# Four graph layers in fp32: layer normalisation folded into centred weight matrices and PSUM evictions

## The chip, the cores and the metric

The kernel runs on one core of a Trainium2 chip. The metric is the device time of one execution in microseconds; the figure used is the median of the runs shown. Engines are named as in the profile: PE is TensorE's matmul stream and PEld its weight loads, DVE is VectorE, ACT is ScalarE, POOL is GpSimd, SP is SyncE, which here issues most of the DMA transfers. PSUM is the memory that TensorE writes its products to; other engines read ("evict") it from there.

## The reference

Everything is fp32. There are N = 2708 rows with D = 256 columns in `x` and a weighted adjacency matrix `adj` of N x N. Four layers follow each other, each a graph step and a feed-forward step, both on a layer normalisation without parameters and both added back:

```python
def _layernorm(x, axis=-1, eps=1e-5):
    m = jnp.mean(x, axis=axis, keepdims=True)
    v = jnp.var(x, axis=axis, keepdims=True)
    return (x - m) / jnp.sqrt(v + eps)

x = x + gnn(_layernorm(x), adj)        # layers 0 to 3
x = x + ffn(_layernorm(x))
```

- Layer 0: `gnn` is `weights @ (x @ W + B)`, weights an exponential of adj; `ffn` is a mixture of 8 experts, top 2, hidden size 1024.
- Layer 1: `gnn` is `relu(A @ (x @ W) + b)` with `A = adj + I`, its entry (i, j) scaled by deg_i and deg_j, deg being one over the root of the row sum; `ffn` is one hidden layer of 1024 and one of 8 output matrices for each row.
- Layer 2: `gnn` is a one-head graph attention: `h = x @ W.T`, scores `a_src[j] + a_dst[i]`, leaky ReLU, softmax over the neighbours, `elu(w @ h)`; `ffn` has routed experts of hidden size 512 and a layer normalisation with gamma and beta of its own at its end.
- Layer 3: `gnn` is the same with 4 heads of 64 columns; `ffn` is a linear map, `x @ weight.T + bias`.

With the row's mean m and rstd = 1/sqrt(v + eps), a normalised row times a matrix W is rstd * ((x - m) @ W). It is also rstd * (x @ C), where C is W with the mean of each of its columns taken off, because x @ C = x @ W - m * (column sums of W). Both kernels compute the same values in exact arithmetic.

## The kernel before

`x` stays on the chip as 22 tiles of 128 rows (the last has 20). TensorE contracts over partitions, so each tile must be turned before a product with a weight matrix: two transposes of 128 x 128 (one for each half of the 256 columns, `DC` = 2) into PSUM (line L203), and one copy out of it on ACT (L204), all in `turn_to`. `times` then issues the products of a tile (L246; an fp32 matmul leaves two records). Tiles go through in `FOURS`: the first two, then five groups of four. `stats` gives mean and variance of a group (L176, L177 on DVE) and, with `by_log`, rstd by a logarithm and an exponential on ACT (L141). `shift` makes nb = -mean * rstd (L195). ACT then writes the normalised tile xn = rstd * x + nb.

Where this stands in the program, in order of time:

- **Layer 0** (0 to 612 us). Its first weight matrix is already centred, by two products with a matrix of ones and two DVE steps (L821 to L826). Its `x` goes in without xn. The graph product is L891; experts follow (L587 to L689).
- **Layer 1's front** (613.7 to 672). `norm_project` goes through FOURS. `both` loads the two expert outputs of two tiles ("both", from DRAM, in the four places of the tag "adrow" in pool `gp`), and DVE adds them to x (L1037). Then stats, shift, xn (L215), transposes and copy, products, and ACT's eviction to `sup` with scale `deg` (L1100). The graph product follows, L1164: for each of 22 row blocks of adj a load (L1129, tag "adrow"), a mask (L1133), the diagonal (L1136, L1137), and products into PSUM `acc`. `Units` (the experts) own three places `hs` in one tile of the pool `hw`, set to zero at the start (L621), into which rows are gathered (`fetch_rows`, L638).
- **Layer 2's front** (1140 to 1176.5). For each four: a load "mine" and the add (L1284), `norm_stretch` (L229 to L240, xn L235), products with `w_l2` (256 columns and two score columns), a copy of the scores (`sc`, L1293), row scores turned and sent through DRAM (L1208, L1210), exponentials, and `hh` = product times an exponential (L1301, DVE). The attention product is L1367, with weights `e` from DVE (L1361).
- **Layer 3's parts** (1400 to 1590). The feed-forward step of layer 2 goes over parts of up to four tiles: hidden L353 and L355, `outputs` L1550 to L1554. One part later `finish` normalises y, applies gamma and beta, adds to x (L1566, L1584 to L1586), takes the statistics of x and writes the normalised x into `y` (L1579); `front` turns it, multiplies by `wa` (256 + 8 columns) and evicts three pieces on ACT (L1604 to L1606). The last part's finish and front are written as a generator, `last_stretch`, that is worked off step by step inside the attention (`waiting`, L1741).
- **Layer 3's attention** (1590 to 1951). For slots of (turn, row block): DVE makes e (L1753), PE multiplies into num (L1783) and den (L1793). `closing`, another generator, finishes 16 tiles inside it: ELU, statistics, xn (L1727), the last product with `wf`, bias and x (L1735, L1736), and the output's DMA. `close` and `last` do it for the last six tiles after the attention (`norm_stretch`, POOL's bias add L1676, o L1680, DMA L1681).

Each engine works off its own queue in order. The builder chooses the order of the instructions in a queue, within the program's data dependences; `behind`, `pin`, `after` and `add_manual_dep` add to these by hand. The adds of `both` are held behind the last entry of `shifts` in this way.

Of the kernel before, what the change touches and what calls it, by code (L numbers as in the profile page):

```python
# [8 lines left out]
F32 = mybir.dt.float32  # L9
# [57 lines left out]
def adj_ffn4(ctx: ExitStack, tc: tile.TileContext, a: dict, out: bass.AP):  # L67
# [138 lines left out]
    def norm_project(pool, w_sb, emit, ahead=None, by_log=False):  # L206
        for tiles in FOURS:
            if ahead is not None:
                ahead(tiles)
            st = stats(tiles, by_log=by_log)  # L210
            nb = shift(st, len(tiles))
            for i, t in enumerate(tiles):
                r = rows(t)
                xn = work.tile([P, D], F32, name="xn")[:r]
                s.activation(xn, x[:r, t, :], AF.Identity, scale=st[1][:r, i : i + 1],  # L215
                             bias=nb[:r, i : i + 1])
                xT = pool.tile([P, DC, P], F32, name="xT", bufs=3)
                turn_to(xT[:, :, :r], xn, r)
                emit(t, r, times(xT, 0, r, w_sb, D))
# [6 lines left out]

    def norm_stretch(xT, c0, w, by_log=False):

        own = tiles_of(c0, w)  # L229
        st = stats([t for t, _, _ in own], by_log=by_log)  # L230
        nb = shift(st, len(own)) if by_log else None
        for i, (t, k, r) in enumerate(own):
            xn = work.tile([P, D], F32, name="xn")[:r]
            if by_log:
                s.activation(xn, x[:r, t, :], AF.Identity, scale=st[1][:r, i : i + 1],  # L235
                             bias=nb[:r, i : i + 1])
            else:
                norm_to(xn, t, i, st)
            turn_to(xT[:, :, k : k + r], xn, r)
        return own  # L240
# [369 lines left out]
    class Units(Blocks):  # L610
# [3 lines left out]
        def __init__(self, pool, given, weights, hidden):  # L614
# [5 lines left out]
            self.hs = pool.tile([P, 3, HC * P], F32, name="hs")  # L620
            g.memset(self.hs, 0.0)  # L621
# [12 lines left out]
        def fetch_rows(self):  # L634
            m, n = self.named.pop(0)
            h = self.hs[:, self.places[1] % 3, :]
# [112 lines left out]
    with ExitStack() as l0:  # L749
# [71 lines left out]
        p = ps_tmp()  # L821
        for c in range(DC):
            te.matmul(p[:, :D], lhsT=all_ones, rhs=w_sb[:, c, :], start=(c == 0), stop=(c == DC - 1))
        for c in range(DC):
            v.scalar_tensor_tensor(w_sb[:, c, :], p[:, :D], -1.0 / D, w_sb[:, c, :], op0=ALU.mult,
                                   op1=ALU.add)  # L826
# [26 lines left out]
        for tiles in GROUPS:  # L853
# [8 lines left out]
            for j in range(FULL):  # L862
# [5 lines left out]
                if begin and j % 2 == 0:  # L868
                    for t0 in (j,) if j < FULL - 3 else (j, j + 2) if j == FULL - 3 else ():
                        front(t0)  # L870
# [127 lines left out]
    with ExitStack() as l1:  # L998
# [25 lines left out]
        def both(tiles):  # L1024

            for t0 in tiles[::2]:
                two = range(t0, min(t0 + 2, tiles[-1] + 1))
                o = gp.tile([P, 2, 2 * D], F32, name="both", tag="adrow", bufs=4)
# [18 lines left out]
        def send1(tiles):  # L1047
# [44 lines left out]
            for i, t in enumerate(tiles):  # L1092
# [6 lines left out]
        norm_project(gp, w_l1,  # L1099
                     lambda t, r, p: s.activation(sup[:r, t, :], p, AF.Copy,  # L1100
                                                  scale=deg[:r, t : t + 1]), both, True)
# [89 lines left out]
        def beside(b):  # L1191
            if b == NA + 4:
# [5 lines left out]
                score_columns(w_l2, D, ad_bc, 1, D + 1)  # L1198

# [38 lines left out]
    with tc.tile_pool(name="t3", reuse_waits="tile", bufs=1) as t3:  # L1238
# [29 lines left out]
        with tc.tile_pool(name="g2", reuse_waits="tile", bufs=1) as gp:  # L1268
# [5 lines left out]
            for tiles in FOURS:  # L1274
# [11 lines left out]
                own = norm_stretch(xT, t0 * P, (n - 1) * P + rows(tiles[-1]), True)  # L1286
# [4 lines left out]
                for i, (t, k, r) in enumerate(own):  # L1291
                    ps.append(times(xT, k, r, w_l2, D + 2, ps_acc()))
                    s.copy(sc[:r, i, :], ps[-1][:, D:])  # L1293
# [6 lines left out]
                for p, (t, k, r) in zip(ps, own):  # L1300
                    v.tensor_scalar(hh[:r, t, :D], p[:, :D], hh[:r, t, D :], None, op0=ALU.mult)  # L1301
# [51 lines left out]
            for n in (5, 5, 5, 4, 2):  # L1353
# [18 lines left out]
                if c0 == 0:  # L1372
                    score_columns(wa, D, row_bc(work, "L3_gnn_a_r", D, "elu_e"), NH, D)
                    score_columns(wa, D, row_bc(work, "L3_gnn_a_l", D, "elu_e"), NH, D + NH)

# [124 lines left out]
        with tc.tile_pool(name="h2", reuse_waits="tile", bufs=2) as hp:  # L1500
# [56 lines left out]
            def finish(own, y, by_log=False):  # L1557
# [17 lines left out]
                st = stats(tiles, by_log=by_log)  # L1575
                yield
                nb = shift(st, len(own))
                for i, (t, q0, r) in enumerate(own):
                    s.activation(y[:r, i, :], x[:r, t, :], AF.Identity, scale=st[1][:r, i : i + 1],  # L1579
                                 bias=nb[:r, i : i + 1])  # L1580
# [7 lines left out]
            def front(own, y, c0, w):  # L1588

                sc = gp.tile([P, 4, NH], F32, name="sc", bufs=1)  # L1590
# [3 lines left out]
                def turn(i, r):  # L1594
                    xTs.append(gp.tile([P, DC, P], F32, name="xT3", bufs=3))
                    turn_to(xTs[i][:, :, :r], y[:r, i, :], r)

                turn(0, own[0][2])
                for i, (t, k, r) in enumerate(own):
# [4 lines left out]
                    s.copy(wh[:r, t, :, :DK], p[:, :D].rearrange("p (h d) -> p h d", h=NH))  # L1604
                    s.copy(wh[:r, t, :, DK], p[:, D : D + NH])
                    s.copy(sc[:r, i, :], p[:, D + NH :])  # L1606
# [14 lines left out]
            for c0, w in parts:  # L1621
# [9 lines left out]
                if was is not None:  # L1631
                    at_once(finish(*was[:2], end))
                y = ypool.tile([P, 4, D], F32, name="y", bufs=2)
                outputs(own, hT, y)
                if was is not None:
                    at_once(front(*was))
                    for t in range(NT) if was[2] == 0 else ():
# [4 lines left out]
                was = (own, y, c0, w)  # L1642
        sums.close()

        with tc.tile_pool(name="g3e", reuse_waits="tile", bufs=1) as ge, ExitStack() as sums:
# [22 lines left out]
            def last(tiles):  # L1668

                for g0 in range(0, len(tiles), 4):  # L1670
# [3 lines left out]
                    own = norm_stretch(xT, c0, some[-1] * P + rows(some[-1]) - c0, True)  # L1674
                    for t, k, r in own:
                        g.tensor_tensor(x[:r, t, :], x[:r, t, :], bf[:r], ALU.add)  # L1676
                    for t, k, r in own:
                        p = times(xT, k, r, wf, D)
                        o = work.tile([P, D], F32, name="o")
                        v.tensor_tensor(o[:r], p, x[:r, t, :], ALU.add)  # L1680
# [201 lines left out]
```

## Time and profile before

| what | us |
|---|---|
| median of 3 runs (1965.44 to 1976.37) | 1967.63 |
| the profiled execution | 1973.19 |
| its span, first to last instruction | 1971.4 |
| busy: PE / PEld | 1859.3 / 1349.5 |
| busy: DVE / ACT / POOL | 1087.3 / 678.5 / 324.3 |
| L203 to L246, the front of layer 1 | 621.5 to 672.0 |
| first L1284 to first L1367, the front of layer 2 | 1140.4 to 1176.5 |
| last L1550 to first L1783 | 1581.3 to 1590.2 |
| last attention product to the end of the span | 1950.7 to 1971.4 |

The profile is of one execution, so its parts add up to its own time, 1973.19 us. Busy time counts the time in which an engine executes, not that in which it waits for another. The chain of waits follows the work that ended last back from the end: what stands on it sets the time. The clock granted to TensorE varies between half and full speed, and a product takes about twice as long at half: four records of L246 in layer 1's front took 2.09 us at 0.50 and 1.13 to 1.14 at 1.00.

### The profile page before, as it was taken

How to read it: one execution, taken by the hardware profiler on the slowest of the kernel's cores; microseconds unless marked ns; L12 is line 12 of the kernel's file. 1: busy time of each engine (PE TensorE's matmuls, PEld its weight loads, DVE VectorE, ACT ScalarE, POOL GpSimd, SP SyncE). 2: the span in 40 equal slices, each digit the busy share in tenths (PEclk: the TensorE clock that was granted, in tenths of full speed). 3: DMA queues.
4: the chain of work that ended last, by engine and by line, in shares of the span. 5: the costliest groups of instructions: out<-in, count | busy, mean ns of one | idle time of the engine just before them, and what ended most of it. 6: DMA issues, size and time to landing. Idle time of an engine off the chain costs nothing.

```text
span 1971.4 us, 26038 instructions
## 1 busy us (share of the span) xinstructions
PE 1859.3 (94%) x9613; PEld 1349.5 (68%) x9613; DVE 1087.3 (55%) x2460; ACT 678.5 (34%) x1560; POOL 324.3 (16%) x361
## 2 busy tenths in 40 slices
PE   7999989999997999999897879999899999999997
PEld 6888778888886788888786758888566732232343
DVE  7686852543334324443441165456364399899896
ACT  7878832222223303113131261224243452032232
POOL 1005363333321000201436400000000000000000
PEclk9999989999996999999898989999899999999999
DMA  8536477887753352533758830000101000000000
GB/s 270 153 98 170 130 260 277 324 319 267 292 226 121 107 155 98 146 104 114 232 181 275 306 87 1 1 1 1 43 1 33 17 1 23 22 11 28 20 20 15
DMA packets 87141, 243.95 MB, mean 124 GB/s; under 512 B 17139, under 2 KB 41163, under 8 KB 77792
## 3 DMA queue, kind: packets, MB, share of 16 engines
q1 hardware_dynamic: 70048, 197.09, 30.2%
q0 software_dynamic: 16960, 45.12, 6.8%
q8 instruction: 79, 1.29, 0.3%
q14 instruction: 54, 0.44, 0.1%
HBM read 216.29 MB, written 28.71 MB: 124 GB/s over the span
## 4 chain that ended last, share of the span: by engine, by line
PE 73%; DMA 11%; DVE 7%; issue 4%; ACT 3%; POOL 1%; SPq 0%; POOLq 0%; DVEq 0%; ACTq 0%
PE num L1783 10%; PE ps_acc L1367 9%; PE acc L1164 8%; PE ps_tmp L353 8%; PE acc L891 7%; PE den L1793 5%; PE ps_acc L587 5%; PE yacc L597 5%; PE ps_tmp L246 4%; DMA given<-ys,xs 4%; PE ps_acc L1550 3%; DMA given<-ys,names 1%; DMA hs<-hid,names 1%; PE ps_tmp L203 1%; PE yacc L688 1%
## 5 line engine op out<-in xcount | busy, mean ns | idle before, releaser
L1753 DVE SCALAR_TENSOR_TENSOR e<-arena,G,mask 128x1024 f32<-128x1024 f32 (+1 forms) x264 | 287.7, 1148 | 18.3 <-PE den L1793 18.3
L1783 PE MATMUL num<-e,wh 128*64 128x512 f32 (+4 forms) x1056 | 214.9, 551 | 0.3 <-ACT L_gnn_W L1210 0.3
L1367 PE MATMUL ps_acc<-hh,e 128*128 128x257 f32 x882 | 199.2, 382 | 1.7 <-ACT o L1312 1.7
L1164 PE MATMUL acc<-sup,adrow 128*128 128x256 f32 x882 | 199.6, 383 | 1.1 <-DMA adrow<-in_adjT 1.1
L891 PE MATMUL acc<-msg,wt 128*128 128x256 f32 x882 | 197.7, 381 | 1.9 <-DVE wt L851 1.2
L1164 PEld LDWEIGHTS acc<-sup,adrow 128*128 128x128 f32 x882 | 166.0, 191 | 28.7 <-issue 4.9
L1367 PEld LDWEIGHTS ps_acc<-hh,e 128*128 128x128 f32 x882 | 163.6, 190 | 29.3 <-ACT o L1312 4.7
L891 PEld LDWEIGHTS acc<-msg,wt 128*128 128x128 f32 x882 | 164.9, 190 | 27.2 <-DVE wt L851 2.1
L589 ACT ACTIVATE hTs<-ps_acc,wa 128x256 f32<-128x256 f32 (+1 forms) x192 | 88.8, 466 | 245.9 <-PE yacc L597 166.8
L587 PE MATMUL ps_acc<-xTs,wa 128*128 128x256 f32 (+1 forms) x768 | 170.8, 375 | 1.9 <-DVE xTs L560 1.8
L597 PE MATMUL yacc<-wb,hTs 128*128 128x256 f32 x736 | 167.4, 380 | 1.8 <-DVE ys L599 1.8
L587 PEld LDWEIGHTS ps_acc<-xTs,wa 128*128 128x128 f32 x768 | 137.5, 191 | 28.9 <-DVE xTs L560 5.4
L1783 PEld LDWEIGHTS num<-e,wh 128*64 128x64 f32 (+1 forms) x1056 | 66.3, 136 | 127.6 <-issue 108.0
L597 PEld LDWEIGHTS yacc<-wb,hTs 128*128 128x128 f32 x736 | 137.5, 190 | 20.1 <-DVE ys L599 2.5
L1361 DVE SCALAR_TENSOR_TENSOR e<-Rb,G,mask 128x640 f32<-128x640 f32 (+2 forms) x110 | 85.1, 774 | 92.8 <-PE ps_acc L1367 92.7
L204 ACT COPY xT<-ps_tmp 128x256 f32<-128x256 f32 x120 | 41.8, 364 | 229.5 <-PE ps_tmp L203 228.9
L1793 PE MATMUL den<-e,wh 128*32 128x512 f32 (+4 forms) x1056 | 118.0, 548 | 0.0
L1133 DVE TENSOR_SCALAR mask<-adrow 128x1024 uint8<-128x1024 f32 (+1 forms) x66 | 41.4, 629 | 127.9 <-DMA adrow<-in_adjT 127.7
L688 PE MATMUL yacc<-wb,hTs 128*128 128x256 f32 x384 | 94.4, 397 | 7.9 <-DMA wb<-in_L_ffn_Wdp 7.5
L688 PEld LDWEIGHTS yacc<-wb,hTs 128*128 128x128 f32 x384 | 74.1, 200 | 19.9 <-issue 4.8
L851 DVE SCALAR_TENSOR_TENSOR wt<-adrow,wt 128x640 f32<-128x640 f32 (+3 forms) x67 | 71.0, 1062 | 29.3 <-ACT wt L141 29.0
L1793 PEld LDWEIGHTS den<-e,wh 128*32 128x32 f32 (+1 forms) x1056 | 30.2, 108 | 77.9 <-issue 73.8
(446 smaller groups left out, 2632.4 us busy)
## 6 DMA issues: line engine op xcount, KB each, us to landing
adhalf<-in_adjT SPq DMA_DIRECT2D x42, 677.0 KB
wb<-in_L_ffn_W2p SPq DMA_DIRECT2D x24, 1152.0 KB
wb<-in_L_ffn_Wdp SPq DMA_DIRECT2D x24, 1152.0 KB
wa<-in_L_ffn_W1b SPq DMA_DIRECT2D x24, 1028.0 KB
adrow<-in_adjT SPq DMA_DIRECT2D x42, 512.0 KB
adrow<-in_adjT SPq DMA_DIRECT2D x42, 320.0 KB
adrow<-in_adjT SPq DMA_DIRECT2D x21, 576.0 KB
hid<-hrow POOLq DMA_DIRECT2D x21, 512.0 KB, 3.6
```

Source lines behind the costliest of these rows:

```text
L353: te.matmul(p[:, :w], lhsT=w1[:, c, f * P : (f + 1) * P], rhs=xnT[:, c, c0 : c0 + w], start=(c == 0), stop=(c == DC - 1))
L587: te.matmul(p[:, f % 2, : m * P], lhsT=w1[:, c, f * P : (f + 1) * P], rhs=xT[:, c, : m * P], start=(c == 0), stop=(c == DC - 1))
L589: s.activation(hT[:, f, : m * P], p[:, f % 2, : m * P], AF.Gelu, bias=bias[:, f : f + 1])
L597: te.matmul(q[:, k, :], lhsT=hT[:, f, k * P : (k + 1) * P], rhs=w2[:, f, :], start=(f == 0), stop=(f == HC - 1))
L688: te.matmul(q, lhsT=hT[:, f, :], rhs=w2[:, f, :], start=(f == 0), stop=(f == HC - 1))
L891: te.matmul(p[:q, n - pair[0], :], lhsT=wt[:, k : k + q], rhs=msg[:r, j, :], start=(j == 0 and n == pair[0]), stop=(j == FULL - 1 and n == ...
L1164: te.matmul(p[:q, n - pair[0], :], lhsT=ad[:, k : k + q], rhs=sup[:r, j, :], start=(j == 0 and n == pair[0]), stop=(j == FULL - 1 and n == ...
L1361: v.scalar_tensor_tensor(e[:r, :w], Rb[:r, c0 : c0 + w], G[:r, j, :], mask[:r, j, c0 : c0 + w], op0=ALU.max, op1=ALU.mult)
L1367: te.matmul(p[:, : D + 1], lhsT=e[:, k : k + q], rhs=hh[:, j, :], start=(j == 0), stop=False)
L1753: v.scalar_tensor_tensor(e[:, :w], slow[:, m % 2, k, :w], G[:, j, 2 * pair + k, :], mask[:, j, c0 : c0 + w], op0=ALU.max, op1=ALU.mult)
L1783: te.matmul(num[k * DK : (k + 1) * DK, hf, :q], lhsT=wh[some, j, 2 * pair + k, :DK], rhs=e[some, h0 - c0 : h0 - c0 + q], start=(j == 0), s ...
L1793: te.matmul(den[z : z + Q, :q], lhsT=wh[some, i, 2 * pair + k, DK : DK + 1] .to_broadcast([some.stop - some.start, Q]), rhs=e[some, h0 - c ...
```

## The change

1. `norm_project` becomes `project`. It transposes x itself, two tiles into one PSUM bank, with one ACT copy for both (512 wide), ahead of the statistics. `by` = rstd * deg (DVE) is the scale of the eviction to `sup`. xn and nb go.
2. The centring of layer 0 becomes a function, `centre`, and is also used for the matrices of layer 1 (`w_l1`, inside layer 0's graph product), layer 2 (`w_l2`, among layer 1's units), layer 3 (`wa`, at the start of layer 2's product) and the last one (`wf`, in a generator that starts at slot 19 of the attention).
3. `hs` becomes three tiles with the tag "hs" in `hw`, and `both` loads into that tag; "adrow" is used by rows of adj only.
4. Layer 2's front turns x itself; the scores are evicted with scale rstd, and `hh` takes rstd as a second factor.
5. `finish` no longer writes the normalised x; `front` turns x, and its three evictions are scaled by rstd.
6. `last` and `closing` turn x; rstd is a factor in the step that makes o. In `closing`, mean and xn go.

The diff, cut to its core:

```diff
-    def norm_project(pool, w_sb, emit, ahead=None, by_log=False):
+    def project(pool, w_sb, scale, ahead, emit):
         for tiles in FOURS:
-            if ahead is not None:
-                ahead(tiles)
-            st = stats(tiles, by_log=by_log)
-            nb = shift(st, len(tiles))
+            ahead(tiles)
+            t0, G = tiles[0], len(tiles)
+            turned = []
+            for i in range(0, G, 2):
+                xT = pool.tile([P, DC, 2 * P], F32, name="xT", bufs=2)
+                p = ps_tmp()
+                r = rows(t0 + i + 1)
+                for k in range(2):
+                    q = rows(t0 + i + k)
+                    for c in range(DC):
+                        te.transpose(p[:, (c * 2 + k) * P : (c * 2 + k) * P + q],
+                                     x[:q, t0 + i + k, c * P : (c + 1) * P], ident[:q, :q])
+                s.copy(xT[:, :, : P + r], p.rearrange("p (c t) -> p c t", c=DC)[:, :, : P + r])
+                turned.append(xT)
+            st = stats(tiles, by_log=True)
+            by = small.tile([P, G], F32, name="by", tag=f"by{G}", bufs=2)
+            shifts.append(v.tensor_tensor(by, st[1], scale[:, t0 : t0 + G], ALU.mult).ins.name)
             for i, t in enumerate(tiles):
                 r = rows(t)
-                xn = work.tile([P, D], F32, name="xn")[:r]
-                s.activation(xn, x[:r, t, :], AF.Identity, scale=st[1][:r, i : i + 1],
-                             bias=nb[:r, i : i + 1])
-                xT = pool.tile([P, DC, P], F32, name="xT", bufs=3)
-                turn_to(xT[:, :, :r], xn, r)
-                emit(t, r, times(xT, 0, r, w_sb, D))
+                emit(t, r, times(turned[i // 2], i % 2 * P, r, w_sb, D), by[:r, i : i + 1])
+
+    def centre(w):
+        n = w.shape[2]
+        p = ps_tmp()
+        for c in range(DC):
+            te.matmul(p[:, :n], lhsT=all_ones, rhs=w[:, c, :], start=(c == 0), stop=(c == DC - 1))
+        for c in range(DC):
+            v.scalar_tensor_tensor(w[:, c, :], p[:, :n], -1.0 / D, w[:, c, :], op0=ALU.mult,
+                                   op1=ALU.add)
...
-            self.hs = pool.tile([P, 3, HC * P], F32, name="hs")
-            g.memset(self.hs, 0.0)
+            self.hs = [pool.tile([P, HC * P], F32, name="hs", tag="hs", bufs=3) for _ in range(3)]
+            for h in self.hs:
+                g.memset(h, 0.0)
...
                 if begin and j % 2 == 0:
+                    if j == 6:
+                        centre(w_l1)
...
-                o = gp.tile([P, 2, 2 * D], F32, name="both", tag="adrow", bufs=4)
+                o = hw.tile([P, 2, 2 * D], F32, name="both", tag="hs", bufs=3)
...
-        norm_project(gp, w_l1,
-                     lambda t, r, p: s.activation(sup[:r, t, :], p, AF.Copy,
-                                                  scale=deg[:r, t : t + 1]), both, True)
+        project(gp, w_l1, deg, both,
+                lambda t, r, p, by: s.activation(sup[:r, t, :], p, AF.Copy, scale=by))
...
                 score_columns(w_l2, D, ad_bc, 1, D + 1)
+                centre(w_l2)
...
-                own = norm_stretch(xT, t0 * P, (n - 1) * P + rows(tiles[-1]), True)
+                own = tiles_of(t0 * P, (n - 1) * P + rows(tiles[-1]))
+                for t, k, r in own:
+                    turn_to(xT[:, :, k : k + r], x[:r, t, :], r)
+                rstd = stats(tiles, by_log=True)[1]
...
-                    s.copy(sc[:r, i, :], ps[-1][:, D:])
+                    s.activation(sc[:r, i, :], ps[-1][:, D:], AF.Copy, scale=rstd[:r, i : i + 1])
...
-                for p, (t, k, r) in zip(ps, own):
-                    v.tensor_scalar(hh[:r, t, :D], p[:, :D], hh[:r, t, D :], None, op0=ALU.mult)
+                for i, (p, (t, k, r)) in enumerate(zip(ps, own)):
+                    v.tensor_scalar(hh[:r, t, :D], p[:, :D], rstd[:r, i : i + 1], hh[:r, t, D :],
+                                    op0=ALU.mult, op1=ALU.mult)
...
                     score_columns(wa, D, row_bc(work, "L3_gnn_a_l", D, "elu_e"), NH, D + NH)
+                    centre(wa)
...
-                st = stats(tiles, by_log=by_log)
-                yield
-                nb = shift(st, len(own))
-                for i, (t, q0, r) in enumerate(own):
-                    s.activation(y[:r, i, :], x[:r, t, :], AF.Identity, scale=st[1][:r, i : i + 1],
-                                 bias=nb[:r, i : i + 1])
+                rstd.append(stats(tiles, by_log=by_log)[1])
                 yield
...
-                    turn_to(xTs[i][:, :, :r], y[:r, i, :], r)
+                    turn_to(xTs[i][:, :, :r], x[:r, own[i][0], :], r)
...
-                    s.copy(wh[:r, t, :, :DK], p[:, :D].rearrange("p (h d) -> p h d", h=NH))
-                    s.copy(wh[:r, t, :, DK], p[:, D : D + NH])
-                    s.copy(sc[:r, i, :], p[:, D + NH :])
+                    one = by[:r, i : i + 1]
+                    s.activation(wh[:r, t, :, :DK], p[:, :D].rearrange("p (h d) -> p h d", h=NH),
+                                 AF.Copy, scale=one)
+                    s.activation(wh[:r, t, :, DK], p[:, D : D + NH], AF.Copy, scale=one)
+                    s.activation(sc[:r, i, :], p[:, D + NH :], AF.Copy, scale=one)
...
-                    own = norm_stretch(xT, c0, some[-1] * P + rows(some[-1]) - c0, True)
+                    own = tiles_of(c0, some[-1] * P + rows(some[-1]) - c0)
+                    by = stats(some, by_log=True)[1]
+                    for t, k, r in own:
+                        turn_to(xT[:, :, k : k + r], x[:r, t, :], r)
...
-                        v.tensor_tensor(o[:r], p, x[:r, t, :], ALU.add)
+                        v.scalar_tensor_tensor(o[:r], p, by[:r, i : i + 1], x[:r, t, :], op0=ALU.mult,
+                                               op1=ALU.add)
...
-                v.scalar_tensor_tensor(mv[:q, 0:1], mv[:q, 0:1], -1.0, mv[:q, 1:2], op0=ALU.mult,
-                                       op1=ALU.mult)
-                xn = work.tile([P, D], F32, name="xn")[:q]
-                s.activation(xn, x[:q, t, :], AF.Identity, scale=mv[:q, 1:2], bias=mv[:q, 0:1])
-                yield
                 xT = gp.tile([P, DC, P], F32, name="xT3", bufs=3)
-                turn_to(xT[:, :, :q], xn, q)
+                turn_to(xT[:, :, :q], x[:q, t, :], q)
...
-                v.tensor_tensor(o, p, bf[:q], ALU.add)
+                v.scalar_tensor_tensor(o, p, mv[:q, 1:2], bf[:q], op0=ALU.mult, op1=ALU.add)
...
+            def centred():
+                centre(wf)
+                yield
...
-            scores, active, waiting = {}, [], [(1, last_stretch())]
+            scores, active, waiting = {}, [], [(1, last_stretch()), (19, centred())]
```

## The prediction

> **What bounds the kernel now.** I read the page first (engine shares, the forty slices), then the chain of waits, then tables by stretch for the places that the diff touches.
>
> ```profile
> PE 1859.3 (94%) x9613; PEld 1349.5 (68%) x9613; DVE 1087.3 (55%) x2460; ACT 678.5 (34%) x1560; POOL 324.3 (16%) x361
> PE   7999989999997999999897879999899999999997
> PEclk9999989999996999999898989999899999999999
> PE 73%; DMA 11%; DVE 7%; issue 4%; ACT 3%; POOL 1%; SPq 0%; POOLq 0%; DVEq 0%; ACTq 0%
> ```
>
> TensorE is busy for 94% of the span and carries 73% of the chain. So ACT work that the diff deletes (88 normalisations of 0.6 us, 53 us in all) is worth its own time nowhere in general; it counts where TensorE waits. Slice 13 (591 to 641 us) has the lowest clock of all, 0.6: there the front of layer 1 begins. The stretches of that front (columns: PE, PEld, DVE, ACT, POOL busy, clock, DMA share, GB/s):
>
> ```profile
> 620.00:628.00 8.00, 5.50 (x13) 3.33 (x14) 5.49 (x17) 4.11 (x11) 0.00 (x0) 0.50 0.83 282
> 628.00:636.00 8.00, 6.50 (x17) 4.17 (x17) 6.74 (x22) 4.95 (x13) 0.00 (x0) 0.50 0.59 167
> 640.00:644.00 4.00, 2.93 (x12) 2.00 (x12) 2.22 (x5) 2.92 (x8) 0.00 (x0) 0.79 0.00 0
> 644.00:652.00 8.00, 5.57 (x27) 3.93 (x26) 6.00 (x23) 5.33 (x14) 0.00 (x0) 1.00 0.56 168
> 660.00:668.00 8.00, 8.00 (x43) 6.61 (x42) 1.21 (x3) 4.57 (x12) 0.00 (x0) 1.00 0.22 66
> ```
>
> TensorE had half its clock until 640 and gaps until 652; from 660 it never waits. Why it waits is in the chain (start, length, what):
>
> ```profile
> 629.03 2.09 PE ps_tmp L246 x4
> 631.14 0.47 ACT sup L1100
> 631.61 0.33 ACT xT L204
> 631.95 0.04 issue
> 631.99 2.09 PE ps_tmp L246 x4
> ...
> 1582.65 1.48 ACT y L1579 x3
> 1584.12 0.27 ACT xT L204
> 1584.43 2.13 PE ps_tmp L246 x4
> ...
> 1958.60 0.61 ACT xn L235
> 1959.20 0.04 issue
> 1959.25 0.69 PE num L203 x2
> ```
>
> One tile is product, eviction, copy of the next transposes, product: 2.96 us at half clock, 1.95 at full. The other two places show TensorE behind a normalisation: at the end of layer 3's parts and at the kernel's end.
>
> **Layer 1's front (L1037, L215, L203, L246).** Removed: 22 xn (603 ns each on ACT) and five nb (163 ns). Moved: transposes go ahead of the statistics, two tiles share one copy, so products no longer alternate with one copy and one eviction. Added: five small multiplications (`by`). Work per four tiles: DVE 2.49 (adds) + 2.2 (statistics) + 0.16, and in the new order also the mask, ident and diag of an adj row (0.69 + 0.29 + 0.23) ahead of `by`: about 6.1, 6.5 with waits. TensorE at full clock takes 4 x (0.87 + 0.22) = 4.4, at half 8.7; ACT 4 x 0.47 + 2 x about 0.6 = 3.1. With DVE as the limit, the five `by` after 621.3 end at about 629, 635, 641.5, 647 and 652.6 and the last sup at 655.2. Of the products L1164 the old order holds 34 records (17 products, 0.435 us each) inside the front, the new one 5; so 12 x 0.435 = 5.2 us must be added for the same point: 660.4 against 672.0, a gain of 11.6. The added wait is that of sup for `by`; behind it on ACT stand the next pair's copy and so the next transposes, and the products' PSUM banks stay taken: four banks serve both, so TensorE stalls when DVE is some two tiles late, which is why I let DVE set the pace. Bounds: 4 if DVE waits for the first adj rows, 16 if it never does.
>
> SP's order: both0 to 3, adj row 0, both4 and 5, row 1 and so on. `both` gets three places of its own instead of four shared ones; each load waits for the add three loads earlier. Old transfers ended by 640 at up to 282 GB/s, and both are read in tile order, so I cost this at nothing; if that cover fails, a load takes 3.98 us (the first one) and shifts the chain by part of that. The memsets of the units' three `hs` tiles now wait for the last adds, on POOL (2.7 us); behind them are only gathers needed near 757, so nothing. After the front TensorE is the limit (8.00 of 8).
>
> *The clock.* The trace shows 0.50 for 28 us although PE was busy for 69 to 88% of each stretch; in layer 2's front 0.50 became 0.65 and 1.00 within about 4 us, during four transposes and eight products without a gap. [...]
>
> **Layer 2's front (L1284, L1293, L1301; 1140.4 to 1176.5).** 22 xn and nb go; transposes start after the adds at 1141.1 instead of 1143.5 (2.4 us). The cycle per four tiles is 5.7 us (L1208 at 1153.66, 1159.49, 1165.16). DVE then has 1.25 + 2.27 + 1.8 (hh) = 5.3 of it. DVE's hh of the last tiles are queued behind the first e's, with the first product waiting; that is inside the lower bound. hh takes a second factor inside the same instruction, and sc a scale (its copy is 170 ns; bound -0.02 to +0.1 each). First product 1173.7 instead of 1176.5: gain 3 (1 to 5).
>
> **Layer 3's parts (1403 to 1590).** TensorE runs back to back through 13.7 us of L353 and 13.8 of L1550, and the y at L1579 hide beside it; deleting them gives nothing there. The three evictions per tile become scaled activations. The nearest rows:
>
> ```profile
> L1604 ACT COPY wh<-ps_tmp 128x256 f32<-128x256 f32 x19 | 7.0, 370 | 8.6 <-PE ps_tmp L246 8.6
> L1100 ACT ACTIVATE sup<-ps_tmp,deg 128x256 f32<-128x256 f32 x21 | 10.0, 474 | 18.9 <-PE ps_tmp L246 18.9
> ```
>
> So +0.1 for the large one, and for the two small ones between nothing and +0.1. TensorE waits 0.64 to 1.33 us before L1208 for these evictions; +0.2 to 0.5 a front, five fronts: a loss of 1.5 (1 to 2.5). At the last part, TensorE idles from 1581.28 to 1583.19 for y: x is complete on DVE at 1580.2, so 1.9 come back; the following products run at half clock (2.13), and part of 2.5 more comes with a shorter idle time. Late next is rstd for the eviction, near 1582.2. Gain 3.5 (2 to 4.4). The last stretch inside the attention waits 1.65 us (1613.9 to 1615.5) for the same y, but DVE is full there (9.8 of 10): gain 1 (0 to 1.7).
>
> **Attention and closing.** From 1640 to 1945 PE is busy 20.00 in every 20 us. Sixteen closings lose 601 ns of ACT and 152 of DVE; beside a full TensorE that is nothing, and DVE's e (15 to 19.8 of 20) doesn't need it back.
>
> **The end (L235 to L1680).** PE stops at 1950.7, transposes began at 1959.25. Now they take x as it is finished, 1952.3 to 1956.6; products from about 1955.5, two at half clock (1.8) and four at 0.87: about 1962.6. POOL's six bias adds (0.73 each) must follow the statistics, 1957.5 to 1961.9, and each o waits for its own. The last o starts at 1963 instead of 1968.18: gain 5 (2.5 if the clock stays at 0.5, 7 if POOL keeps up).
>
> **Centring.** Four matrices, each two products (0.9 us) and two DVE steps (0.45). w_l1, wa and wf stand where PE has no gap: +0.9, +0.9, +1.2 with the wait for a PSUM bank; w_l2 stands where TensorE waits for weights: 0 to +0.9. Loss 3.3 (2.7 to 4.3).
>
> **Sum.** -11.6 - 3 + 1.5 - 3.5 - 1 - 5 + 3.3 = -19.3 us on the profiled execution, 1973.19 (span 1971.4 and 1.8 around it), hence 1953.9. That execution lies 5.6 above the median, 1967.63; my forecast is 1967.63 - 19.3 = 1948.3.
>
> **Rivals.** *(1) Layer 1's front is not shorter.* Masks precede `by` on DVE, `both` has three places, and evictions wait for `by`: every four tiles could take the old 7.8 us (1.95 x 4) and the first sup come no earlier. For it: a DVE wait of 5.1 us stood at 636 to 641, and the first mask now stands inside the front. Against it: that wait came from ACT's queue, which loses its xn. Only the other terms remain, -7.7: 1960. *(2) The half clock stays (slower).* Runs of transposes, then short runs of products: TensorE at 0.5 through layer 1's front to 669.5, five L1164 products inside it at 0.87 (4.4) and twelve behind (10.4): 684.3 against 672.0, +12.3. The same in layer 2 (25 us of TensorE work become 50 from 1141.5): +15 instead of -3. Sum -19.3 + 11.6 + 12.3 + 3 + 15 = +22.6: 1990. It decides if the clock is still 0.5 after about 660 in layer 1; confined to layer 1 it makes +4.6, 1972. Against it: the clock rose in the old fronts with more gaps. *(3) The gains are there in full*, bounds together: -16 - 5 + 1 - 4.4 - 1.7 - 7 + 2.7 = -30: 1937. *(4) It doesn't do what it says*: TensorE in the front is held by transfers. They need 5.5 MB, about 20 us at 282 GB/s, and end near 638: not the limit; it would look like (1).
>
> **How the numbers follow.** A measurement of this kernel can tell about 0.5%, 9.8 us. Forecast as summed (1943 to 1956) 0.58, (3) 0.20, (1) with (4) 0.15, (2) 0.07. Faster by over 9.8 us (below 1957.8): the first two and a little of (1), 0.79; the same: the rest of (1) and (2) confined to layer 1, 0.15; slower 0.06. The range 1936 to 1965 reaches from (3) over (1) and leaves out (2).
>
> **What would show it.** Layer 1: clock above 0.9 by 632, no gap of TensorE over 1 us after 645, continuous L1164 by 655; if instead DVE waits for adrow ahead of `by`, (1). Layer 2: first L1367 near 1159 on a clock shifted by the earlier gains (36.1 us after the first add now, 33.3 then). Layer 3: L1604's successor near 470 ns, L203 right behind L1550. End: last o about 12 us behind PE's last attention product, not 17.5. Wrong if fronts shorten and the sum doesn't move, or the clock stays at 0.5.

## The result, and the profile after

The changed kernel takes 1956.12 us (median of 7 runs, 1953.86 to 1958.66), the kernel before 1971.43 us in the runs beside them (7 runs, 1965.44 to 1978.39). The ratio is 0.9921, 95% interval 0.9900 to 0.9941: faster by 15 us, 12 to 20. Run again later beside other kernels it came to 0.9936 (0.9916 to 0.9957). The profiled execution took 1954.26 us, span 1952.5.

The page after, its lines that answer to those shown of before:

```profile
PE 1858.9 (95%) x9629; PEld 1350.7 (69%) x9629; DVE 1091.6 (56%) x2438; ACT 642.9 (33%) x1461; POOL 324.1 (17%) x363
PE   7999989999999999999897889999899999999998
PEclk9999989999998999999898999999899999999999
PE 73%; DMA 12%; DVE 5%; issue 5%; ACT 2%; POOL 2%; SPq 0%; POOLq 0%; DVEq 0%; ACTq 0%
```

TensorE does the same work (1858.9 us busy against 1859.3) in a shorter span, ACT 36 us less. In the thirteenth slice PE's digit went from 7 to 9 and the clock from 0.6 to 0.8: this is layer 1's front. The same stretches as before, of the changed kernel (columns: PE, PEld, DVE, ACT, POOL busy, clock, DMA share, GB/s):

```profile
620.00:628.00 8.00, 7.00 (x28) 5.48 (x28) 6.23 (x20) 3.47 (x9) 0.00 (x0) 0.72 0.97 354
628.00:636.00 8.00, 7.96 (x42) 6.23 (x42) 7.97 (x25) 5.26 (x13) 0.00 (x0) 1.00 0.85 290
640.00:644.00 4.00, 3.64 (x21) 2.99 (x20) 3.93 (x17) 2.48 (x6) 0.95 (x1) 1.00 0.28 88
644.00:652.00 8.00, 8.00 (x40) 6.01 (x40) 3.98 (x16) 4.71 (x12) 1.91 (x2) 1.00 0.00 0
```

From 628 TensorE is at full clock and full but for one gap of 0.36 us at 640; before, that began at about 656 (3.39 of 4 us busy from 652 to 656). Its queue in this time (start, length, line):

```profile
619.55 1.09 PE L219 MATMUL ps_tmp<-ident,x 128*128 128x128 f32 x4 [2.00 <-DVE x L1039]
621.39 3.50 PE L250 MATMUL ps_tmp<-L_gnn_W,xT 128*128 128x256 f32 x8 [0.76 <-ACT xT L221]
624.73 1.04 PE L219 MATMUL ps_tmp<-ident,x 128*128 128x128 f32 x8
626.01 3.72 PE L250 MATMUL ps_tmp<-L_gnn_W,xT 128*128 128x256 f32 x16 [0.24 <-ACT xT L221]
```

Products come in runs of a whole group, with no eviction between them that TensorE waits for. To see where the 18.8 us between the two profiled spans come from, I compare stages by the distance between the starts of two fixed instructions (lines of the kernel before; records counted from 0), and put beside them the mean over the profiles of all kernels below that have the part (five to nine profiles) or don't have it (five; for layer 1's front two):

| stage, from and to | before | after | mean without | mean with |
|---|---|---|---|---|
| layer 1's front: first add of both to record 100 of L1164 | 68.66 | 52.27 | 67.9 | 53.0 |
| layer 2's front: first L1284 to first L1367 | 36.07 | 33.05 | 36.5 | 33.5 |
| layer 3's parts: first L353 to last L1550 | 177.19 | 178.07 | 176.4 | 177.2 |
| last part: last L1550 to first L1783 | 9.26 | 6.28 | 8.2 | 6.3 |
| attention: first to last L1783 | 356.34 | 359.83 | 356.5 | 359.9 |
| end: last L1783 to the end of the span | 24.87 | 21.97 | 24.9 | 22.0 |

(Kernels that change a stage in another way are left out of its means.) Layer 1's front is all but the whole. What layer 2's front, the last part and the end gain by the means, 7.8 us, is mostly given back: 3.4 in the attention, 0.7 in layer 3's parts and 0.8 inside layer 2's product, where `wa` is centred. In layer 3 the scaled evictions are dearer than the copies were (rows of the parts, columns count | busy us, mean ns):

```profile
L1610 ACT ACTIVATE wh<-ps_tmp,rs_y 128x256 f32<-128x256 f32 x16 | 7.5, 471 | 4.6 <-PE ps_tmp L250 4.2
L1613 ACT ACTIVATE sc<-ps_tmp,rs_y 128x4 f32<-128x4 f32 x16 | 4.3, 268 | 0.0
L1612 ACT ACTIVATE wh<-ps_tmp,rs_y 128x4 f32<-128x4 f32 x16 | 4.2, 263 | 0.0
```

They were 370, 181 and 175 ns. At the last part, the chain no longer holds a normalised y:

```profile
1565.65 0.09 ACT var L141
1565.74 0.26 ACT xT L204
1566.00 0.04 issue
1566.05 1.17 PE ps_tmp L250 x4
```

### The profile page after: what moved, and what is told of

It reads as the page before. It is cut to its first block, busy times and chain, and to the rows that moved or that the text cites. A ratio compares the mean times of both kernels' runs of the same rounds, so it can differ in the third digit from the quotient of the medians.

```text
span 1952.5 us, 25928 instructions
## 1 busy us (share of the span) xinstructions
PE 1858.9 (95%) x9629; PEld 1350.7 (69%) x9629; DVE 1091.6 (56%) x2438; ACT 642.9 (33%) x1461; POOL 324.1 (17%) x363
## 4 chain that ended last, share of the span: by engine, by line
PE 73%; DMA 12%; DVE 5%; issue 5%; ACT 2%; POOL 2%; SPq 0%; POOLq 0%; DVEq 0%; ACTq 0%
PE num L1793 10%; PE ps_acc L1373 9%; PE ps_tmp L357 8%; PE acc L893 7%; PE acc L1165 7%; PE den L1803 6%; PE ps_acc L591 6%; PE yacc L601 5%; PE ps_tmp L250 3%; PE ps_acc L1557 3%; DMA given<-ys,xs 3%; DMA given<-ys,names 2%; DMA adrow<-in_adjT 1%; PE ps_tmp L203 1%; DMA hs<-hid,names 1%
## 5 line engine op out<-in xcount | busy, mean ns | idle before, releaser
L1367 DVE SCALAR_TENSOR_TENSOR e<-Rb,G,mask 128x640 f32<-128x640 f32 (+2 forms) x110 | 85.1, 774 | 93.1 <-PE ps_acc L1373 93.0
L204 ACT COPY xT<-ps_tmp 128x256 f32<-128x256 f32 x98 | 33.5, 364 | 258.4 <-PE ps_tmp L203 242.8
```

The costliest lines, as they stand in the source:

```text
L1367: v.scalar_tensor_tensor(e[:r, :w], Rb[:r, c0 : c0 + w], G[:r, j, :], mask[:r, j, c0 : c0 + w], op0=ALU.max, op1=ALU.mult)
```

## Experiments

Times are ratios to the kernel before on the same chip. A stage of 1 to 3 us is below what the times tell, so for those I read the stage in the profile; the times decide only on layer 1's front.

**1. Layer 1's part alone, and everything but it.** The first kernel is before with `project`, `centre(w_l1)` and the places; the second is the changed one with this undone:

```diff
-        project(gp, w_l1, deg, both,
-                lambda t, r, p, by: s.activation(sup[:r, t, :], p, AF.Copy, scale=by))
+        norm_project(gp, w_l1,
+                     lambda t, r, p: s.activation(sup[:r, t, :], p, AF.Copy,
+                                                  scale=deg[:r, t : t + 1]), both, True)
...
-                    if j == 6:
-                        centre(w_l1)
...
-                o = hw.tile([P, 2, 2 * D], F32, name="both", tag="hs", bufs=3)
+                o = gp.tile([P, 2, 2 * D], F32, name="both", tag="adrow", bufs=4)
```

> The kernel before with only layer 1's part of the change: project, by, w_l1 centred, and both in places of its own. Theory A (layer 1's front carries the gain): the count of L1164 products reached by any time after the front is some 16 us earlier than before, and the whole kernel about 15 us shorter (ratio near 0.992). Theory B (the gain is spread over the four stages): half of it, 7 to 9 us.

> The changed kernel with layer 1's front as before (xn, shared places, w_l1 not centred); all else changed. Theory A: the stages of layers 2 and 3 and the end give -3, -2, +3.5 in the attention and -3 at the end by the two profiles, so about 3 to 4 us shorter than before (ratio 0.998). Theory B: 8 us or more shorter.

Measured: layer 1's part alone 0.9924 (0.9893 to 0.9954), its front 52.81 us; all the rest 0.9999 (0.9981 to 1.0016), its front 67.05. Theory A holds: layer 1 carries the time. The rest nets to nothing that can be measured: by the stage table it would be about -3 us (-7.8 and +4.9, as above), inside the interval.

**2. The places of `both` without project, and project without the places.**

```diff
-                o = gp.tile([P, 2, 2 * D], F32, name="both", tag="adrow", bufs=4)
+                o = hw.tile([P, 2, 2 * D], F32, name="both", tag="hs", bufs=3)
```

The first kernel makes this edit (and `hs` three tiles) in the kernel before; the other takes it back in the changed one.

> The kernel before with both in three places of its own, hs as three tiles, and nothing else. If the places carry the front's gain (adj rows arrive early, so TensorE has L1164 products to put between the front's), the end of the front comes 8 us or more earlier. If the alternation of eviction, xn and copy on ACT carries it, 0 to 3 us: TensorE still waits for ACT after each tile and still runs at half clock to about 640.

> The changed kernel with both loaded into the four places of adrow again. If the places carry the gain, it gives 8 us or more of the 16 back. If project carries it, 0 to 3 us are given back: adj rows can't be loaded before the last loads of both, so the mask doesn't stand ahead of by any more, and fewer L1164 products fall into the front; the clock is still full by about 625.

Measured: places alone 0.9938 (0.9920 to 0.9957), front 55.05 us; project alone 0.9910 (0.9892 to 0.9928), front 53.43. Neither expectation holds as a whole: each edit by itself gives nearly all of it (13.6 and 15.2 of the 16.4 us). They aren't parts of a sum but two ways to the same end. The queue of TensorE with the places alone, the old xn and the old alternation still there:

```profile
633.33 0.38 PE L203 MATMUL ps_tmp<-ident,xn 128*128 128x128 f32 x2
633.55 1.03 PE L1165 MATMUL acc<-sup,adrow 128*128 128x256 f32 x4
634.41 1.04 PE L246 MATMUL ps_tmp<-L_gnn_W,xT 128*128 128x256 f32 x4
635.29 0.38 PE L203 MATMUL ps_tmp<-ident,xn 128*128 128x128 f32 x2
635.50 1.03 PE L1165 MATMUL acc<-sup,adrow 128*128 128x256 f32 x4
636.37 1.04 PE L246 MATMUL ps_tmp<-L_gnn_W,xT 128*128 128x256 f32 x4
```

A tile takes 1.96 us as before, but the time in which TensorE waited for eviction and copy holds two products of the graph step, for which the rows of adj are now there (0.87 us by the starts): the first mask of a row is made at 627.4 instead of 652.3. The front ends as late as before (last sup 671.8 against 672.5), with 89 records of L1164 behind it instead of 37. With project there are no waits to fill: the front ends at 651.3 with 13 records done. Either way TensorE is full (from 628 to 636 busy for 8.00 of 8 us with the places alone, 7.96 in the changed kernel), and the second edit finds nothing left to win.

**3. The clock by itself.** Seven products without use in the kernel before, where TensorE waits for the first loads:

```diff
+        idle = ps_tmp()
+        for _ in range(7):
+            i = te.matmul(idle[:, :D], lhsT=all_ones, rhs=w_l1[:, 0, :], start=True, stop=True)
+            tc.add_manual_dep(i.ins, sums_done, mybir.DependencyInfo(
+                mybir.DependencyClass.NoSync, mybir.DependencyReason.DATA), reason="order")
         norm_project(gp, w_l1,
```

> The kernel before with seven idle products (all_ones by w_l1, 256 columns, result unused, about 6 us at half clock) put between the sums of L979 and the first transposes, where TensorE waits for both anyway. Theory C (the half clock is what made the old front long; both places and project shorten it because they keep TensorE busy): full clock soon after 622, 1.95 instead of 2.96 us for the tiles that ran at half, 7 to 8 us gained, and the kernel 0.3 to 0.4% shorter. Theory D (the waits for ACT between tiles are the loss, the clock is a by-product): the gaps remain, DVE's or ACT's pace shows, 0 to 3 us.

Measured: 1.0014 (0.9995 to 1.0033); the front is 66.41 us, 2.2 shorter. TensorE's queue:

```profile
616.87 5.96 PE L1102 MATMUL ps_tmp<-L_gnn_W,all_ones 128*128 128x256 f32 x14
622.66 0.38 PE L203 MATMUL ps_tmp<-ident,xn 128*128 128x128 f32 x2
623.50 1.13 PE L246 MATMUL ps_tmp<-L_gnn_W,xT 128*128 128x256 f32 x4 [0.46 <-ACT xT L204]
...
628.28 0.44 PE L203 MATMUL ps_tmp<-ident,xn 128*128 128x128 f32 x2 [1.69 <-ACT xn L215]
629.18 2.07 PE L246 MATMUL ps_tmp<-L_gnn_W,xT 128*128 128x256 f32 x4 [0.46 <-ACT xT L204]
```

The products took 1.13 us from the first tile on, so the clock did rise early; after the wait of 1.69 us for xn they were at 2.07 again for two tiles and at 1.53 for a third. Half clock lasted 17.1 us in all instead of 30.7, as long as with the places alone, and only 2.2 of the 13.6 us came of it. (The idle products held the first transposes back by 0.7 us, from 3.9 to 4.6 behind the first add.) Theory D holds: the waits are the loss. From 636 the tiles run at 1.96 us with a wait of 0.61 in each, at full clock. What a clock that stays full from the start would give was not tried.

**4. Order or xn.** The kernel before with the transposes of a group ahead of its products, two tiles to a copy, xn still made on ACT:

```diff
-                xT = pool.tile([P, DC, P], F32, name="xT", bufs=3)
-                turn_to(xT[:, :, :r], xn, r)
-                emit(t, r, times(xT, 0, r, w_sb, D))
+                    for c in range(DC):
+                        te.transpose(p[:, (c * 2 + k) * P : (c * 2 + k) * P + q],
+                                     xn[:, c * P : (c + 1) * P], ident[:q, :q])
+                s.copy(xT[:, :, : P + r], p.rearrange("p (c t) -> p c t", c=DC)[:, :, : P + r])
+                turned.append(xT)
+            for i, t in enumerate(tiles):
+                r = rows(t)
+                emit(t, r, times(turned[i // 2], i % 2 * P, r, w_sb, D))
```

> The kernel before with only the order of layer 1's front changed: statistics, nb and xn on ACT stay, w_l1 isn't centred, both stays in the shared places; but two tiles' transposes share a bank and one copy, and come ahead of the group's products. Theory E (project gains because transposes and copies no longer alternate with products and evictions): ACT becomes the pace with 0.60 + 0.47 + about 0.3 = 1.37 us a tile, 30 us for 22 tiles instead of 43 (1.96 each): about 10 us of the 15 that project gains. Theory F (the gain is that xn is gone, and transposes can start before the statistics): 0 to 4 us.

Measured: 0.9991 (0.9977 to 1.0005); the front 63.31 us, 5.3 shorter. This is between the two theories: of the 15.2 us of project about a third comes of the order, and the rest of taking xn away, with which the transposes also move ahead of the statistics. The third is rough: the fronts of two profiles of the old code differ by 1.6 us (68.66 and 67.05), and the time shows 1.8 us, at most 4.5 by its interval. The table by stretch shows what is left:

```profile
620.00:628.00 8.00, 4.96 (x12) 3.10 (x12) 5.29 (x19) 3.57 (x10) 0.00 (x0) 0.50 0.90 305
628.00:636.00 8.00, 7.52 (x21) 5.39 (x22) 4.32 (x16) 4.89 (x13) 0.00 (x0) 0.53 0.39 140
```

TensorE still waits for the statistics and xn in the first 8 us (4.96 busy against 7.00), and half clock lasts to 635.5 (0.53 in the second row) instead of 624.5.

**5. What the centrings cost.**

```diff
-                    if j == 6:
-                        centre(w_l1)
...
-                centre(w_l2)
...
-                    centre(wa)
...
-            scores, active, waiting = {}, [], [(1, last_stretch()), (19, centred())]
+            scores, active, waiting = {}, [], [(1, last_stretch())]
```

> The changed kernel without the four added centrings (w_l1, w_l2, wa, wf keep their column means, so the rows' means are not taken off). Theory: each costs its two products where TensorE has no gap, by the profile of after 0.8 (wa, between products 100 and 450 of layer 2), 1.06 (wf, at slot 19), up to 0.9 (w_l1), nothing for w_l2: 2.7 us together. Rival: TensorE's queue takes them beside waits, 0 to 1 us.

Measured: 0.9908 (0.9877 to 0.9940), not to be told from the changed kernel by time. In the profile: records 100 and 450 of layer 2's product lie 0.8 us closer together (`wa`: 81.65 against 82.46), the attention is 1.4 us shorter (359.83 to 358.43), and a lag of 1.05 us that the changed kernel takes between records 80 and 160 of layer 0's product is absent. The theory holds place by place, with 2.9 us for the three that could be read (1.05, 0.8 and, for `wf`, the 1.06 by which L1783's successor falls behind at slot 19 in the changed kernel and not here; the other 0.35 of the attention's 1.4 stand in the last stretch). `w_l2` stands among waits for loads and couldn't be read. Layer 0 as a whole was no shorter all the same: this profile and the two of experiment 8, all three with `project` but without `w_l1`'s products in layer 0, have a half-clock stretch of 3.4 us at 114 to 115 us, and the 26 records of the graph product behind it take 7.57 us instead of 5.88. The gap before it is one of 0.49 us that stands in the changed kernel too, so why the clock fell is not shown.

**6. The attention's loss.** One empty step more in `closing` and in `finish`:

```diff
                 rstd.append(stats(tiles, by_log=by_log)[1])
                 yield
+                yield
...
+                yield
                 xT = gp.tile([P, DC, P], F32, name="xT3", bufs=3)
                 turn_to(xT[:, :, :q], x[:q, t, :], q)
```

> The changed kernel with one empty step more in closing and in finish, so that transposes, products and first steps of neighbouring closings fall into the slots of before. Theory: the attention lost 2.4 us in its two rows of closings because a closing's transposes and the next one's first step now share a slot, and TensorE waits for ACT to free one of two PSUM banks (0.5 us waits before L1713); with the step back, the 2.4 us return (lag constant from product 384 to 936). Rival: the loss comes of rstd as a second factor on DVE, and it stays.

Measured: 0.9940 (0.9913 to 0.9967), again no difference in time; but the lead of the attention's products over before is constant from record 384 to 768 (23.1 us throughout) and 23.5 at the end, where in the changed kernel it had shrunk from 18.3 to 16.9 and then 15.9. So the 2.4 us of the closings are back. The attention takes 357.90 us instead of 359.83, only 1.9 less, because the step in `finish` cost 0.8 in the last stretch (records 0 to 128). The step in `closing` alone was not tried. TensorE's groups in 100 us among the first closings, first of the changed kernel:

```profile
L203 PE MATMUL ps_tmp<-ident,x 128*128 128x128 f32 x14 | 3.1, 301 | 0.0
L1713 PE MATMUL ps_tmp<-ident,oT 128*128 128x128 f32 x12 | 2.5, 291 | 0.5 <-ACT xT L204 0.5
```

and with the step:

```profile
L203 PE MATMUL ps_tmp<-ident,x 128*128 128x128 f32 x16 | 3.5, 300 | 0.0
L1714 PE MATMUL ps_tmp<-ident,oT 128*128 128x128 f32 x12 | 2.3, 273 | 0.0
```

The wait for ACT's copy before L1713 is gone. The change had taken a normalisation out of `closing` and with it a step, so the transposes of some tiles moved into the slot of a neighbour's first step. In the changed kernel's queue (first step L1713, L1714):

```profile
1717.82 0.44 PE L203 MATMUL ps_tmp<-ident,x 128*128 128x128 f32 x2
1718.09 0.38 PE L1713 MATMUL ps_tmp<-ident,oT 128*128 128x128 f32 x2
1718.31 0.27 PE L1714 MATMUL ps_tmp<-ident,arena 128*128 128x128 f32 x1
```

Before, and again with the step, L203 stands alone in its slot, and a neighbour's last product stands where L203 does here. The wait for a PSUM bank comes twice in the attention, 0.46 us each time, so it is 0.9 of the 2.4 us; the rest shows no idle time of TensorE, and what makes it is open. That the step brings all of it back while rstd is still a factor on DVE speaks against the rival.

**7. The end.** The changed kernel with the last six tiles as before:

```diff
-                    own = tiles_of(c0, some[-1] * P + rows(some[-1]) - c0)
-                    by = stats(some, by_log=True)[1]
-                    for t, k, r in own:
-                        turn_to(xT[:, :, k : k + r], x[:r, t, :], r)
+                    own = norm_stretch(xT, c0, some[-1] * P + rows(some[-1]) - c0, True)
...
-                        v.scalar_tensor_tensor(o[:r], p, by[:r, i : i + 1], x[:r, t, :], op0=ALU.mult,
-                                               op1=ALU.add)
+                        v.tensor_tensor(o[:r], p, x[:r, t, :], ALU.add)
```

> The changed kernel with the last six tiles as before (x normalised on ACT, then transposed). Theory: the last o starts 5.2 us later behind the last attention product (21.7 us instead of 16.5), and since 2.3 us of this were lost behind it (landing of the last transfers, POOL's answer at the end of the program), the span is 3 to 5 us longer. Rival: the transposes and products of the end keep half clock either way and only 1 to 2 us come of it.

Measured: 0.9940 (0.9924 to 0.9955). The last o starts 22.2 us behind the start of the last L1783 (its line before) instead of 16.5, and the end is 25.51 us long instead of 21.97: 3.5 us, as the theory has it.

**8. Combined.** The changed kernel with the empty steps of 6, `centre(w_l1)` moved to where TensorE waits for the first `both`, and the last o in tiles of their own; then the same with `both` in the shared places; then the changed kernel again beside them.

```diff
+        centre(w_l1)
         project(gp, w_l1, deg, both,
...
-                        o = work.tile([P, D], F32, name="o")
+                        o = ge.tile([P, WIDE], F32, name="e", bufs=8)[:, :D]
                         v.scalar_tensor_tensor(o[:r], p, by[:r, i : i + 1], x[:r, t, :], op0=ALU.mult,
```

> The changed kernel with three edits that the runs point to: the two empty steps (2.5 us by their profile), w_l1 centred right before layer 1's front, where TensorE waits 2 us for both (0.9), and the last six o in tiles of their own, so that the fourth needn't wait for the first one's transfer (0.9, of which the end may give back a part). About 4 us shorter than the changed kernel, some 19 to 20 us shorter than before (ratio 0.990). Rival: what is gained in the attention only is real, 2.5 us.

> The same with both in the shared places of adrow. If places and project are substitutes, as the two profiles say, it is within 2 us of the one with own places: the front 1 us longer. If own places cost later (rows of adj loaded early collide with both), it is faster by 2 us or more.

> The changed kernel itself beside these on one chip: ratio near 0.992, as in its first runs; the sum of stages -16.4 (layer 1's front), -3 and -1.7 (fronts of layers 2 and 3), -2.9 (end), +3.5 (attention), +1.7 (centrings in layers 0 and 2) gives -18.8, ratio 0.9905.

Measured, on one chip: 0.9919 (0.9892 to 0.9945), 0.9936 (0.9910 to 0.9961) and 0.9936 (0.9916 to 0.9957). No order among the three can be told, so neither the 4 us of the first nor a cost of the places shows in the times. In the profiles the attention's part is there in both (357.97 us), and so is the front (52.34 and 53.40 us); what `w_l1` gave up in layer 0 went to the half-clock stretch named in 5. The edit of the last o failed: the last o starts 19.2 us (19.1 with shared places) behind the last L1783 instead of 16.5, because the builder chose another order, in which ACT's copies come later and TensorE waits for them:

```profile
1949.29 2.04 PE L250 MATMUL num<-L_ffn_weightT,e 128*128 128x256 f32 x4 [2.15 <-ACT e L204]
```

## Why the prediction held, point by point

The forecast was 1948.3 us against 1967.63, a gain of 19.3 (1%); measured are 15 (12 to 20). 1956.12 us lies just outside the 1943 to 1956 given for the sum and inside the whole range. The difference of the profiled executions, 18.9, agrees closely with the sum, but that is partly luck, since errors cancel: layer 1's front gave 4.8 us more than forecast, the attention 3.3 and the end 2.1 less.

- **Layer 1's front: the step was right in kind, its size too small.** Forecast 11.6 us, measured 16.4 between the two profiles and 14.8 between the means. The term that was mis-sized is DVE's pace, 6.5 us for four tiles. After the first `by` at 621.48 (forecast 621.3) they follow at 627.99, 633.10, 638.16, 643.41 and 648.36: 6.5 us once, then 5.1. The last was forecast at 652.6; these 4.2 us are most of the 4.8. I had added up durations of rows as if they didn't overlap; on DVE one starts before the one ahead has ended (an add at 621.56 and a `by` from 621.48 to 621.64). From 627.99 to 633.10 the durations of DVE's 17 rows add up to 6.4 us. The products left out of the front were counted well: 24 records, 5.2 us.
- **What carries it was only half seen.** I took `project` for the cause and costed the places of `both` "at nothing". Experiment 2 shows that the places alone would do nearly the same. Leaving them out did no harm to the number, since the two don't add; I had not foreseen that.
- **The clock.** Forecast: above 0.9 by 632, an estimate of mine from the rise in layer 2's front. Measured: half clock ends at 624.5, 4.9 us after the first transposes and 3.1 after the first products. Rival 2 (1990 us), in which the half clock stays, did not come; no trace of before showed that runs of transposes hold the clock down, and its 669.5 us was an estimate, 22 tiles of 1.74 us of products and 0.44 of transposes, twice their 0.87 and 0.22 at full clock. In the changed kernel a run of eight transposes (1.04 us from 624.73) between groups of products left the clock at 1.00 (624.5 to 640). Whether longer runs would lower it no run here shows.
- **Rival 1** (a group of four takes the old 7.8 us) did not come. Masks did stand ahead of `by` from the second one on (two of them between 626.23 and 627.99), but DVE waited only 0.48 us for a row of adj (with the mean of a tile behind the mask in its queue: statistics ready at 625.67, taken up at 626.84), a group took 5.1 us from then on, and TensorE had groups of products in hand.
- **Layer 2: 3 forecast, 3.0 measured. Layer 3's parts: a loss of 1.5 forecast**, 0.7 measured between the means, with 1.5 between single profiles of the same code; the evictions cost 0.28 us a tile.
- **Last part: 3.5 forecast, 3.0 between the profiles.** Of these only 1.7 are the change: four other profiles that keep the old step have 7.97 to 7.98 us there, the kernel before 9.26, since its clock was at half from 1583.7 to 1587.1, which none of the other four shows at that place. That a shorter idle time brings the clock up there was an estimate of mine that no run shows.
- **Attention: the step that failed.** Forecast were -1 for the last stretch and +1.2 for `wf`, together +0.2; measured +3.5. "Beside a full TensorE that is nothing" looked at DVE and ACT and not at the slots: the yield that went from `closing` cost 2.4 us. `wf` cost the 1.06 that it should. The gain of 1 for the last stretch is only 0.1: its products fall 1.4 us behind by record 64 and have made it good by record 128.
- **The end: 5 forecast, 2.9 measured.** The last o did come 5.2 us sooner. But the last rows of the trace are an exchange between all engines, and POOL joins it at 1951.75, 1.3 us after SP is through; before, it was ready when SP was. POOL's last bias adds, and the row of its DRAIN at the program's end (shortest, median and longest in ns), before and after:

```profile
1962.11 2.08 POOL L1676 TENSOR_TENSOR x<-x,L_gnn_b 128x256 f32<-128x256 f32 x3 [0.73 <-ACT xn L235]
L1878 POOLq DRAIN  x3: 50/109/6953, 1963.0 to 1971.1; - x3
1942.44 3.44 POOL L1686 TENSOR_TENSOR x<-x,L_gnn_b 128x256 f32<-128x256 f32 x5 [1.16 <-DVE st L176]
L1888 POOLq DRAIN  x3: 50/109/7782, 1943.9 to 1952.3; - x3
```

In both profiles the longest DRAIN ends 5.8 us after the last add has ended (1964.19 to 1970.00 before, 1945.89 to 1951.70 after). I had asked of POOL only whether it holds up an o. Its last add came 2.4 us sooner behind the last L1783 (15.3 instead of 17.7), and before it stood 0.5 us under SP: this is the 2.9. Why the DRAIN takes so long, and what bias adds on another engine would give, no run shows.
- **Centrings: 3.3 forecast, 2.9 read.**

## What to carry to other kernels

When an engine waits in short pieces, there are two cures, which here didn't add (13.6 and 15.2 us alone, 16.4 together): take the reason for the wait away, or have other work of that engine ready at that time. Before paying for the first, look whether an operand of the next stage could be there a few microseconds earlier; here giving a load buffers of its own did 13.6 of 16.4 us. When instructions are removed from a hand-stepped generator, look at which steps now fall into one slot, not only at the busy time that is gone. When the end of a program is shortened, look at what each engine still has to finish, not only at the last result.

## What was not expected of the hardware

Layer 1's front ran at half clock for 30.7 us before, 23.9 with the order alone (experiment 4), 17.1 with the places alone, 13.7 in the changed kernel, and 10.2 and then 6.8 with the idle products. A single stretch of 3.4 us moved a stage by up to half its length: the graph product of layer 0 lost 1.7 us in three kernels (experiments 5 and 8), and the last part of layer 3 lost 1.3 in one of five kernels whose code is the same there. A difference of that size between two profiles is no finding until a third has it.
